# Norms by way of DRAM in the first layer and a ring of four pools in the third

## The chip, the cores and the metric

The kernel runs on one core of a Trainium2 chip. The metric is the time of one execution in microseconds on the device; the kernel before has a median of 5616.28 us over three runs (5610.35 to 5618.55). The profiled execution that is read here took 5603.3 us, with a span of 5601.4 us.

## What is computed

The input is a batch of two images of 512 channels and 64 x 64 pixels in float32. Four layers follow one another; each adds to its input what it makes of the group-normalised input.

1. A windowed attention with eight heads of 64 channels. Queries and keys are scaled to unit length per head and pixel; each pixel attends to its 3 x 3 neighbourhood and to 256 pooled tokens.
2. A deformable attention, in which keys and values are sampled at learned offsets.
3. An adaptive pooling. Each channel takes a mixture of its own maximum pools of sizes 1, 3, ... 13; the mixture follows from the channel's mean.
4. A linear attention with random features.

What the change touches is, cut to the core:

```python
# layer 0 (the "first layer")
k_l = k_l / max(norm(k_l), 1e-12)              # per head and pixel; q likewise
attn = softmax(concat([attn_local, attn_pool]))
x_local = einsum(lt, v_local)                  # nine neighbours, lt = learned + softmax weight
x_pool  = einsum(a_pool, v_pool)
# layer 2 (the "third layer")
gap   = mean(x, (2, 3));  s = relu(relu(gap @ w1.T + b1) @ w2.T + b2)
q_s   = clip(floor(s), 0, 5)
out   = frac_b * pools[q_s + 1] + frac_s * pools[q_s] + x
```

## The kernel before, in words

Channels lie on the 128 partitions, in four chunks. An image of 512 channels fills one of two big SBUF buffers; while one holds the image X, the other, Y, is working space.

**First layer (class Local).** The work is cut into 16 units per image: four chunks of 128 channels (two heads each) times four strips of 1024 pixels. `run` (L1739) is a software pipeline: in one turn of its loop, unit u attends (`attend`, L2123), unit u+1 has its tap products and tap sums made (`tap_products`, `tap_sums`) and its values projected, units u+3 and u+4 have queries and keys projected (`projections`), and unit u-1 is weighed (`weigh`, L2203). A tap is one of the nine neighbours. These stages are generators; `in_turn` takes one step of each in rotation. The tile framework then puts each engine's instructions in a fixed order by its own priorities, and every engine works through its list in that order. The transfers of this layer are all issued from one queue, that of SyncE (SP), also in order. "T" is used below for the start of one turn, at its sums of squares.

The norms of a turn come about as follows (`norms`, L1993). The squares of four half strips are summed per head by matmuls with a constant into rows 32s and 32s+1 of one PSUM bank (L2003), and ACT copies the bank to `rows` (L2006). Four transposes (L2010) put pixels on partitions, so that 128 x 32 numbers remain; the DVE takes reciprocal roots with a bit trick and three Newton steps (L2013 to L2024) into the zero-filled tile `wide`; four transposes (L2029) and a copy (L2031) bring them back to rows. `normed` (L2035) spreads each row over 64 partitions by a matmul (L2043) and multiplies the raw keys and queries (L2051). `learned` (L2057) then makes the query that the next turn uses.

The reciprocals of the softmax sums stay in `recip` (L2183). They weight the taps (L2186) and, in `weigh`, the attended values: two matmuls (L2213) spread them over the partitions and the DVE multiplies (L2216). The nine tap weights go to DRAM (`rows`, L2190) and from there to 64 partitions each (`fetch_tap`, L2196, two transfers of 256 KB per tap) into a ring of three buffers. For each tap ACT copies the weights to PSUM (L2223), the DVE multiplies the shifted values (L2226), and GpSimd adds to the output (L2230).

**Third layer.** `pool_weights` (L637, called from L1137) makes the group statistics and the mixture with small operations on the DVE, a power on GpSimd (L99) and a few matmuls. `pool_chunk` (L1140) then goes over the four chunks of channels. Each pool is the 3 x 3 maximum of the one before: a horizontal maximum into h, a vertical one into p (`spread_max`, L683: one DVE operation over 3968 columns, and ACT copies the edges). PE adds each pool, times a diagonal matrix of its weights (L1151), into eight PSUM banks (L1153). Y holds two h and two p buffers, so pool j+2 overwrites pool j. ACT then evacuates the banks and gathers the next layer's statistics (L1183, L1188).

Of the kernel before, what the change touches and what calls it, by code (L numbers as in the profile page):

```python
# [2 lines left out]

# [5 lines left out]
F32 = mybir.dt.float32  # L9
I32 = mybir.dt.int32  # L10
AF = mybir.ActivationFunctionType
ALU = mybir.AluOpType
# [3 lines left out]
P = 128  # L16
C = 512
KC = C // P
# [39 lines left out]
class General:  # L58
# [578 lines left out]
    def pool_weights(self, X, w1, w2, sp, pp, mv=None):  # L637


        nc, vec = self.nc, self.vec  # L640
        nmean, rstd, mv = self.group_stats(X, sp, pp, mv)
        gap = sp.tile([P, KC], F32, name="gap")
        nc.vector.tensor_tensor(gap, mv[:, :, 0], nmean, ALU.add)
        nc.vector.tensor_tensor(gap, gap, rstd, ALU.mult)
        ps = pp.tile([P, TB], F32, name="mm")
        for kc in range(KC):
            nc.tensor.matmul(ps[:32, :1], w1[:, kc, :], gap[:, kc:kc + 1], start=(kc == 0),
                             stop=(kc == KC - 1))
        mid = sp.tile([32, 1], F32, name="mid")
        nc.scalar.activation(mid, ps[:32, :1], AF.Relu, bias=vec[:32, V_B1:V_B1 + 1])  # L650
        ps = pp.tile([P, TB], F32, name="mm")
        for oc in range(KC):
            nc.tensor.matmul(ps[:, oc:oc + 1], w2[:, oc * P:(oc + 1) * P], mid, start=True,
                             stop=True)
        s, q, t, fb, fs = (sp.tile([P, KC], F32, name=f"pw_{n}") for n in ("s", "q", "t", "fb", "fs"))
        nc.vector.tensor_tensor(s, ps[:, :KC], vec[:, V_B2:V_B2 + KC], ALU.add)
        nc.vector.tensor_scalar(s, s, 0.0, None, ALU.max)

        nc.vector.tensor_scalar(q, s, 8.0, None, ALU.min)
        qi = sp.tile([P, KC], I32, name="pw_qi")  # L660
        nc.vector.tensor_copy(qi, q)
        nc.vector.tensor_copy(q, qi)
        nc.vector.tensor_tensor(t, q, s, ALU.is_gt)
        nc.vector.tensor_tensor(q, q, t, ALU.subtract)
        nc.vector.tensor_scalar(q, q, 5.0, None, ALU.min)
        nc.vector.tensor_tensor(fb, s, q, ALU.subtract)
        nc.vector.scalar_tensor_tensor(fs, q, 1.0, s, ALU.add, ALU.subtract)
        wts = sp.tile([P, 7, KC], F32, name="pw_w")
        for j in range(7):
            nc.vector.scalar_tensor_tensor(wts[:, j], q, float(j), fs, ALU.is_equal, ALU.mult)  # L670
            nc.vector.scalar_tensor_tensor(t, q, float(j - 1), fb, ALU.is_equal, ALU.mult)
            nc.vector.tensor_tensor(wts[:, j], wts[:, j], t, ALU.add)
        c0 = sp.tile([P, KC], F32, name="pw_c0")
        d0 = sp.tile([P, KC], F32, name="pw_d0")
        nc.vector.tensor_tensor(d0, fs, fb, ALU.add)
        nc.vector.scalar_tensor_tensor(d0, d0, 1.0, nmean, ALU.add, ALU.mult)
        nc.vector.tensor_tensor(d0, d0, rstd, ALU.mult)
        nc.vector.tensor_tensor(wts, wts, bcast(rstd, 1, 7), ALU.mult)
        nc.vector.tensor_tensor(c0, wts[:, 0], rstd, ALU.add)
        nc.vector.tensor_scalar(c0, c0, 1.0, None, ALU.add)  # L680
        return c0, d0, wts

    def spread_max(self, out, in_, axis):  # L683
# [244 lines left out]
class Net(General):  # L928
# [206 lines left out]
        return w  # L1135

    def pool_weights(self, X, w1, w2, sp, pp):  # L1137
        return super().pool_weights(X, w1, w2, sp, pp, self.mv)

    def pool_chunk(self, X, Y, cc, c0, d0, wts, sp, ppa):  # L1140

# [1 line left out]
        nc = self.nc  # L1143
        x2 = X[:, cc, :]
        img = x2.rearrange("p (y x) -> p y x", x=W)
        tmp = [Y[:, i, :].rearrange("p (y x) -> p y x", x=W) for i in range(KC)]
        accs = [ppa.tile([P, TB], F32, name="acc") for b in range(NB)]

        def add(w, src, j):
# [5 lines left out]

        add(c0[:, cc:cc + 1], x2, 0)
        for j in range(1, 7):
            h, p = tmp[j % 2], tmp[2 + j % 2]
            if j == 1:
                self.spread_max(h, img, 2)  # L1160
                nc.vector.tensor_tensor(h, h, img, ALU.max)
                self.spread_max(p, h, 1)
                nc.vector.tensor_tensor(p, p, h, ALU.max)
            else:

                self.spread_max(h, tmp[2 + (j - 1) % 2], 2)
                self.spread_max(p, h, 1)
            add(wts[:, j, cc:cc + 1], Y[:, 2 + j % 2, :], j)
        mv = self.mv[:, cc]
        if cc == KC - 1:  # L1170

# [488 lines left out]
class Local:  # L1660
# [9 lines left out]
    def __init__(self, net, X, Y, sp_scale, d, wp, yp, pp, ppt, pps):  # L1670
# [4 lines left out]

        self.yd = yp.tile([P, KC, N], F32, name="yd")
        self.wd = yp.tile([3, P, KC, C], F32, name="wd")
        self.rows = cycle([yp.tile([P // 2, self.UT], F32, name=f"rows{i}") for i in range(2)]).__next__

        R = W + 2  # L1680
# [30 lines left out]
        self.w3 = new([P, 3, KC, P], "w3")  # L1711
        self.sq = [new([P, TB], f"sq{i}") for i in range(4)]
        self.half = new([P, 32], "mhalf32")
        self.wide = new([P, NT, P], "wide")
        self.qb = new([P, KC], "qe_scaled")
        self.bias = {i: new([P, KC], "b_" + i) for i in "qkv"}
        self.raw = {"k": self.kraw, "q": self.qn}
# [6 lines left out]
            load(self.raw_w[i], d["W_kv"][:, i * C:(i + 1) * C])  # L1724
        nc.sync.dma_start(self.tok, d["tok32"])
        nc.vector.memset(self.half, -0.5)
        nc.gpsimd.memset(self.wide, 0.0)

        nc.vector.tensor_tensor(self.qb, self.vec[:, V_QE:V_QE + KC], sp_scale, ALU.mult)

# [262 lines left out]
    def norms(self, streams, ended):  # L1993
# [10 lines left out]
                             before[s % len(before)][4], start=True, stop=True)  # L2004
        rows = wp.tile([P, TB], F32, name="n_rows")
        nc.scalar.copy(rows, ps)  # L2006
        yield
        ps = self.bank()
        for t in range(NT):
            nc.tensor.transpose(ps[:, t * P:(t + 1) * P], rows[:, t * P:(t + 1) * P],  # L2010
                                self.net.ident)
        n, y, a = (wp.tile([P, NT, 4, 2], F32, name=f"norms{i}") for i in range(3))
        nc.vector.tensor_scalar(n, ps.rearrange("p (t s r) -> p t s r", t=NT, s=4)[:, :, :, :2],  # L2013
                                1e-24, None, ALU.max)
        yield

        nc.vector.tensor_scalar(y.bitcast(I32), n.bitcast(I32), 1, None, ALU.logical_shift_right)
        nc.vector.tensor_scalar(y.bitcast(I32), y.bitcast(I32), -1, 0x5f3759df, ALU.mult, ALU.add)
        nc.vector.tensor_scalar(n, n, -0.5, None, ALU.mult)
        for i in range(3):  # L2020
            nc.vector.tensor_tensor(a, y, y, ALU.mult)
            nc.vector.tensor_tensor(a, a, n, ALU.mult)
            dst = self.wide.rearrange("p t (s r) -> p t s r", s=4)[:, :, :, :2] if i == 2 else y
            nc.vector.scalar_tensor_tensor(dst, a, 1.5, y, ALU.add, ALU.mult)  # L2024
        yield
        yield
        ps = self.bank()
        for t in range(NT):
            nc.tensor.transpose(ps[:, t * P:(t + 1) * P], self.wide[:, t, :], self.net.ident)  # L2029
        rows = wp.tile([P, TB], F32, name="n_rows")  # L2030
        nc.scalar.copy(rows, ps)  # L2031
        ended += [(s, rows[32 * s:32 * s + 2, :], *a) for s, a in enumerate(before)]
        yield

# [88 lines left out]
    def attend(self, u):  # L2123
# [64 lines left out]
        self.spread = self.rows()  # L2188
        for j in range(2):
            nc.sync.dma_start(self.spread[:, j * TB:(j + 1) * TB], el[j * HD:(j + 1) * HD, :])  # L2190
        self.fetch_tap(0)
        yield
        self.fetch_tap(1)
        yield

    def fetch_tap(self, k):  # L2196

        at = 32 * (k % 2) + 2 * k
        for h in range(2):
            self.nc.sync.dma_start(self.taps[k % 3][h * HD:(h + 1) * HD, :],  # L2200
                                   bcast(self.spread[at + h], 0, HD))

    def weigh(self, u):  # L2203

        nc = self.nc
        cc, y0 = u // self.UN, u % self.UN * self.UY
        out, R = self.out.pop(u), self.recip
        self.fetch_tap(2)
        yield
        banks = [self.bank() for _ in range(2)]  # L2210
        for j, ps in enumerate(banks):
            q = slice(64 * j, 64 * j + 2)
            nc.tensor.matmul(ps, self.cst[q, C_ROW:C_ROW + P], R[q, :], start=True, stop=True)  # L2213
        for j, ps in enumerate(banks):
            o = out[:, j * TB:(j + 1) * TB]
            nc.vector.tensor_tensor(o, o, ps, ALU.mult)  # L2216
        for k in range(9):
            dy, dx = divmod(k, 3)
            parts = [self.taps[k % 3][:, j * TB:(j + 1) * TB] for j in range(2)]

            banks = [self.bank() for _ in range(2)]
            for ps, part in zip(banks, parts):
                nc.scalar.copy(ps, part)  # L2223
            for j, (ps, part) in enumerate(zip(banks, parts)):
                y = y0 + dy + j * self.UY // 2
                nc.vector.tensor_tensor(  # L2226
                    part.rearrange("p (y x) -> p y x", x=W),
                    self.vx[:, y:y + self.UY // 2, dx:dx + W],
                    ps.rearrange("p (y x) -> p y x", x=W), ALU.mult)
            nc.gpsimd.tensor_tensor(out, out, self.taps[k % 3], ALU.add)  # L2230
            if k + 3 < 9:
                self.fetch_tap(k + 3)
            if k < 8:
                yield
        lo = u % self.UN * self.UT
        nc.sync.dma_start(self.yd[:, cc, lo:lo + self.UT], out)
# [162 lines left out]
```

## Time and profile before

The page gives each engine's busy time over the whole span:

| engine | busy us | share | main work |
|---|---|---|---|
| PE (matmul) | 5235.5 | 93% | all projections, attention, pool additions |
| DVE | 3176.3 | 57% | elementwise work, maxima |
| ACT | 1790.9 | 32% | exponentials, copies |
| POOL (GpSimd) | 1811.4 | 32% | additions |
| DMA | | 16.5% of 16 engines | loads, tap weights |

By place in the first image: the first layer ends at about 1150 us of the span, the second at about 1625, the third at about 1910 and the fourth at about 2830; the second image repeats this.

A stage's row in the windows query names an engine's busy time within that stretch. In a timeline, a row's bracket tells how long the engine sat idle ahead of the instruction and which instruction released it. Matmuls in float32 are recorded as two each, so "x8" is four matmuls. Only time on an engine that something later waits for counts toward the end.

### The profile page before, as it was taken

What the parts mean: (1) busy time and instruction counts of PE and PEld (TensorE: products, weight loads), DVE (VectorE), ACT (ScalarE), POOL (GpSimd) and SP (SyncE); (2) the same over time, 40 slices, a digit from 0 to 9 for tenths busy, and PEclk for the clock granted to TensorE, in tenths of its full rate; (3) what the DMA queues carried; (4) which work ended last, traced back from release to release, by engine and by line L of the source; (5) the groups of instructions that cost most, each with busy time, mean ns of one, the idle gap of its engine ahead of it and who ended that gap; (6) DMA issues with size and microseconds to landing.
All of it is one profiled execution on the core that took longest, in us unless ns stands there. A gap on an engine that the chain in (4) does not pass through costs nothing.

```text
span 5601.4 us, 51804 instructions
## 1 busy us (share of the span) xinstructions
PE 5235.5 (93%) x19291; PEld 2262.8 (40%) x19291; DVE 3176.3 (57%) x3816; ACT 1790.9 (32%) x3413; POOL 1811.4 (32%) x1196
## 2 busy tenths in 40 slices
PE   7899999999978899999998999999999789999999
PEld 3433332555323444544343333325543334445443
DVE  3257777745669633544432677777456795334444
ACT  1245555333212233212212455542332122332221
POOL 0025555501310045444400455554012101453443
PEclk9899999999989999999998999999999899999999
DMA  3024444500000000201010344454000000000000
GB/s 138 0 64 119 122 115 136 167 21 24 1 1 0 1 1 1 76 18 36 31 51 2 84 117 116 119 145 143 17 24 1 1 0 1 1 8 14 18 16 24
DMA packets 103353, 276.37 MB, mean 49 GB/s; under 512 B 15090, under 2 KB 28146, under 8 KB 101044
## 3 DMA queue, kind: packets, MB, share of 16 engines
q1 hardware_dynamic: 103092, 272.97, 16.5%
q8 instruction: 154, 2.52, 0.2%
q14 instruction: 107, 0.88, 0.1%
HBM read 224.68 MB, written 48.23 MB: 49 GB/s over the span
## 4 chain that ended last, share of the span: by engine, by line
PE 72%; DVE 15%; issue 5%; DMA 3%; POOL 2%; ACT 2%; SPq 0%; DVEq 0%; ACTq 0%; POOLq 0%
PE mm L133 25%; DVE big L692 6%; PE mm L1330 4%; PE mm L1615 4%; PE mm L1370 4%; PE mm L547 4%; PE mm L1410 2%; PE mm L1226 2%; PE psO L1242 2%; PE psO L1602 2%; PE mm L1631 2%; PE tap L2104 2%; PE mm L1933 2%; POOL late L2230 2%; DMA big<-rows 2%
## 5 line engine op out<-in xcount | busy, mean ns | idle before, releaser
L133 PE MATMUL mm<-big,w 128*128 128x512 f32 x2560 | 1199.2, 613 | 6.5 <-DVE late L2183 5.0
L133 PEld LDWEIGHTS mm<-big,w 128*128 128x128 f32 x2560 | 469.6, 193 | 707.7 <-issue 602.0
L2230 POOL TENSOR_TENSOR late<-late,big 128x1024 f32<-128x1024 f32 x192 | 454.0, 2365 | 335.2 <-DVE big L2226 331.7
L1153 PE MATMUL acc<-big,dg 128*128 128x512 f32 x896 | 408.1, 614 | 79.6 <-DVE big L692 51.2
L692 DVE TENSOR_TENSOR big<-big 128x3968 f32<-128x3968 f32 x96 | 410.8, 4290 | 38.8 <-ACT big L693 16.7
L1232 POOL TENSOR_TENSOR total<-prob 128x512 f32<-128x512 f32 x128 | 159.7, 1270 | 758.4 <-ACT prob L1229 758.4
L1584 POOL TENSOR_SCALAR qf_sum<-qf,ksum_ratio 128x512 f32<-128x512 f32 x128 | 198.8, 1562 | 551.9 <-ACT qf L1634 351.7
L1405 POOL TENSOR_TENSOR big<-big 128x512 f32<-128x512 f32 x224 | 277.4, 1271 | 237.0 <-ACT big L1396 237.0
L2151 POOL TENSOR_TENSOR late<-late 128x512 f32<-128x512 f32 x128 | 160.5, 1275 | 502.5 <-ACT late L2140 477.2
L1609 DVE RECIPROCAL k<-psD 128x512 f32<-128x512 f32 x64 | 214.9, 3357 | 182.6 <-PE psD L1606 182.6
L1153 PEld LDWEIGHTS acc<-big,dg 128*128 128x128 f32 x896 | 174.0, 197 | 312.2 <-issue 282.5
L2223 ACT COPY mm<-big 128x512 f32<-128x512 f32 x384 | 221.7, 594 | 196.6 <-DMA big<-rows 103.3
L1396 ACT ACTIVATE big<-mm,ed 128x256 f32<-128x256 f32 x512 | 194.1, 489 | 278.0 <-DVE top L1392 250.3
L2226 DVE TENSOR_TENSOR big<-big,mm 128x512 f32<-128x512 f32 x384 | 252.4, 680 | 31.9 <-ACT mm L2223 30.9
L2230 POOL TENSOR_TENSOR late<-late,tap 128x1024 f32<-128x1024 f32 x96 | 228.0, 2375 | 122.0 <-DVE norms L2024 72.4
L1330 PE MATMUL mm<-proj,k 64*128 64x256 f32 x2048 | 265.6, 391 | 0.9 <-ACT k L1297 0.9
L1249 DVE RECIPROCAL recip<-psD 128x512 f32<-128x512 f32 x64 | 214.9, 3358 | 87.1 <-PE psD L1246 87.1
L2091 DVE TENSOR_TENSOR prod<-qs,big 128x1024 f32<-128x1024 f32 x192 | 231.0, 1218 | 42.9 <-PE tap L2104 42.6
L1551 DVE TENSOR_REDUCE tops<-mm 128x2 f32<-128x512 f32 x256 | 159.4, 681 | 165.1 <-PE mm L1330 165.0
L1229 ACT ACTIVATE prob<-mm 128x512 f32<-128x512 f32 x256 | 132.0, 604 | 364.4 <-PE mm L1226 359.2
L1330 PEld LDWEIGHTS mm<-proj,k 64*128 64x128 f32 x2048 | 207.8, 188 | 95.0 <-issue 78.7
L1615 PE MATMUL mm<-k,w 128*128 128x512 f32 x512 | 235.6, 602 | 0.0
(352 smaller groups left out, 8384.6 us busy)
## 6 DMA issues: line engine op xcount, KB each, us to landing
big<-rows SPq DMA_DIRECT2D x384, 256.0 KB, 4.0
tap<-rows SPq DMA_DIRECT2D x192, 256.0 KB, 4.1
yd<-late SPq DMA_DIRECT2D x32, 512.0 KB, 4.1
out<-big SPq DMA_DIRECT2D x64, 256.0 KB, 2.0
big<-in_W_kv SPq DMA_DIRECT2D x8, 1024.0 KB, 6.2
rows<-late SPq DMA_DIRECT2D x64, 128.0 KB, 2.4
big<-yd SPq DMA_DIRECT2D x16, 512.0 KB, 4.1
big<-in_x SPq DMA_DIRECT2D x4, 2048.0 KB, 7.6
```

The costliest lines, as they stand in the source:

```text
L133: self.nc.tensor.matmul(ps, w[:, kc, :], X[:, kc, blk * TB:(blk + 1) * TB], start=(kc == 0), stop=(kc == KC - 1))
L547: nc.tensor.matmul(ps, w[:, kc, oc * P:(oc + 1) * P], att[:, kc, :], start=(kc == 0), stop=(kc == KC - 1))
L692: nc.vector.tensor_tensor(o, a, b, ALU.max)
L1153: nc.tensor.matmul(accs[b], dg, src[:, b * TB:(b + 1) * TB], start=(j == 0), stop=(j == 6))
L1330: nc.tensor.matmul(pS[h][i][:, t, :], k[lo:lo + HD, tok:tok + P], proj[lo:lo + HD, :], start=True, stop=True)
L1370: nc.tensor.matmul(ps, X[:, kc, lo:lo + P], wv[:, kc, :], start=(kc == 0), stop=(kc == KC - 1))
L1405: nc.gpsimd.tensor_tensor(a, a, part, ALU.add)
L1615: nc.tensor.matmul(ps, self.wo[:, kc, oc * P:(oc + 1) * P], qs[:, kc, :], start=(kc == 0), stop=(kc == KC - 1))
L2091: self.nc.vector.tensor_tensor(self.prods[k % 3].rearrange("p (y x) -> p y x", x=W), qs, self.kx[:, y + dy:y + dy + self.UY, dx:dx + W], A ...
L2223: nc.scalar.copy(ps, part)
L2226: nc.vector.tensor_tensor(part.rearrange("p (y x) -> p y x", x=W), self.vx[:, y:y + self.UY // 2, dx:dx + W], ps.rearrange("p (y x) -> p y ...
L2230: nc.gpsimd.tensor_tensor(out, out, self.taps[k % 3], ALU.add)
```

## The change

The first layer's norms no longer go through the tensor engine for their change of layout. The rows of sums go to DRAM and come back spread over all 128 partitions as 128 x 32 numbers; the DVE works on them, with two intermediate tiles in PSUM; the results go back to rows by DRAM. The reciprocals of the softmax sums are treated as a tenth tap: row 20 of the weights holds them (the exponential of an empty tap sum is 1, its learned part 0), and they are fetched ahead of the nine others. So eight transposes, one ACT copy and two matmuls per turn disappear; six small transfers, two large ones and two ACT copies are added. The tile `wide` and its memset go.

In the third layer, the pools go round a ring of four buffers (three of Y's and a new one), with a single h. The statistics move from the DVE to ACT and GpSimd, and the maxima from the second pool on are queued behind the last operation of the mixture, in the first chunk. Both are meant to let PE begin its additions sooner and to keep the DVE from waiting for a buffer.

```diff
@@ norms
         rows = wp.tile([P, TB], F32, name="n_rows")
         nc.scalar.copy(rows, ps)
-        yield
-        ps = self.bank()
-        for t in range(NT):
-            nc.tensor.transpose(ps[:, t * P:(t + 1) * P], rows[:, t * P:(t + 1) * P],
-                                self.net.ident)
-        n, y, a = (wp.tile([P, NT, 4, 2], F32, name=f"norms{i}") for i in range(3))
-        nc.vector.tensor_scalar(n, ps.rearrange(...)[:, :, :, :2], 1e-24, None, ALU.max)
-        yield
+        self.flat.reverse()
+        sums, roots = self.flat[0]
+        every = lambda a: a.rearrange("h s (c e) -> (h s c) e", e=32)
+        for h in range(2):
+            nc.sync.dma_start(sums[h], rows[h:P:32, :])
+        n, y = (wp.tile([P, 32], F32, name=f"norms{i}") for i in range(2))
+        nc.sync.dma_start(n, every(sums))
+        yield
+        yield
+        ps = self.bank()
+        m, a = ps[:, :32], ps[:, 32:64]
+        nc.vector.tensor_scalar(m, n, 1e-24, None, ALU.max)
...
         for i in range(3):
-            nc.vector.tensor_tensor(a, y, y, ALU.mult)
-            nc.vector.tensor_tensor(a, a, n, ALU.mult)
-            dst = self.wide.rearrange(...)[:, :, :, :2] if i == 2 else y
-            nc.vector.scalar_tensor_tensor(dst, a, 1.5, y, ALU.add, ALU.mult)
-        yield
-        yield
-        ps = self.bank()
-        for t in range(NT):
-            nc.tensor.transpose(ps[:, t * P:(t + 1) * P], self.wide[:, t, :], self.net.ident)
+            nc.vector.tensor_tensor(a, m, y, ALU.mult)
+            nc.vector.tensor_tensor(a, a, y, ALU.mult)
+            nc.vector.scalar_tensor_tensor(y, a, 1.5, y, ALU.add, ALU.mult)
+        nc.sync.dma_start(every(roots), y)
         rows = wp.tile([P, TB], F32, name="n_rows")
-        nc.scalar.copy(rows, ps)
+        for h in range(2):
+            nc.sync.dma_start(rows[h:P:32, :], roots[h])
@@ fetch_tap, weigh
-        at = 32 * (k % 2) + 2 * k
+        at = 32 * ((i - 1) % 2) + 2 * (i - 1) if i else 20
...
-        banks = [self.bank() for _ in range(2)]
-        for j, ps in enumerate(banks):
-            q = slice(64 * j, 64 * j + 2)
-            nc.tensor.matmul(ps, self.cst[q, C_ROW:C_ROW + P], R[q, :], start=True, stop=True)
-        for j, ps in enumerate(banks):
-            o = out[:, j * TB:(j + 1) * TB]
-            nc.vector.tensor_tensor(o, o, ps, ALU.mult)
-        for k in range(9):
+        for i in range(10):
...
+                if i == 0:
+                    o = out[:, j * TB:(j + 1) * TB]
+                    nc.vector.tensor_tensor(o, o, ps, ALU.mult)
+                    continue
@@ pool_weights (third layer): on ACT instead of the DVE
+        nc.scalar.mul(nmean, ps[:, :KC], -1.0)
+        for kc in range(KC):
+            nc.scalar.activation(col(cent, kc), mv[:, kc, 0:1], AF.Identity, bias=col(nmean, kc))
+        nc.scalar.activation(var, cent, AF.Square)
+        for kc in range(KC):
+            nc.scalar.activation(col(var, kc), col(var, kc), AF.Identity, bias=mv[:, kc, 1:2])
...
+        nc.gpsimd.tensor_tensor(rstd, var, self.mhalf[:, :KC], ALU.pow)
+        for kc in range(KC):
+            nc.scalar.mul(col(gap, kc), col(cent, kc), col(rstd, kc))
@@ pool_chunk
-        tmp = [Y[:, i, :].rearrange("p (y x) -> p y x", x=W) for i in range(KC)]
+        if cc == 0:
+            self.pools = [Y[:, i, :] for i in range(1, KC)] + [sp.tile([P, N], F32, name="pool4")]
+        h = image(Y[:, 0, :])
...
-            h, p = tmp[j % 2], tmp[2 + j % 2]
+            flat = self.pools[(6 * cc + j) % KC]
+            p = image(flat)
...
-                self.spread_max(h, tmp[2 + (j - 1) % 2], 2)
-                self.spread_max(p, h, 1)
+                with self.tc.issue_after(self.mixed) if cc == 0 else nullcontext():
+                    self.spread_max(h, last, 2)
+                    self.spread_max(p, h, 1)
```

## The prediction

> **What bounds the kernel now.** I read the page's chain first, then busy time in windows of 50 us, then the timelines of one unit of the first layer and of the start of the third. The chain by engine, and one window inside the first layer's units (length, then PE, PEld, DVE, ACT, POOL busy, granted clock, DMA):
>
> ```profile
> PE 72%; DVE 15%; issue 5%; DMA 3%; POOL 2%; ACT 2%; SPq 0%; DVEq 0%; ACTq 0%; POOLq 0%
> ```
> ```profile
> 550.00:600.00 50.00, 47.62 (x172) 15.11 (x164) 35.90 (x50) 25.92 (x46) 26.22 (x13) 0.97 0.41 111
> ```
>
> The timeline of a unit on PE (start, length, instruction, idle before it):
>
> ```profile
> 799.62 1.13 PE L2213 MATMUL mm<-late,cst 2*128 2x512 f32 x4
> 800.86 0.66 PE L2010 MATMUL mm<-cst,n_rows 128*128 128x128 f32 x4
> ...
> 814.45 0.63 PE L2029 MATMUL mm<-cst,wide 128*128 128x128 f32 x4 [2.27 <-DVE wide L2024]
> ```
>
> PE ends most of the chain, and in a unit it is busy 47.6 of 50 us. Its one regular hole is 2.27 us ahead of the second set of transposes, L2029, which waits for the DVE's root. A unit without clock loss takes 48.32 us: L2003 starts at 749.25 and at 797.57. Four of 24 take 53.11, three about 50, and the twelve from 351.58 to 942.68 average 49.26. The reason shows in the timeline of a long one:
>
> ```profile
> 368.46 0.63 PE L2029 MATMUL mm<-cst,wide 128*128 128x128 f32 x4 [2.27 <-DVE wide L2024]
> 369.02 3.09 PE L2146 MATMUL mm<-late,vp 128*64 128x512 f32 x8
> ...
> 375.91 5.67 PE L133 MATMUL mm<-big,w 128*128 128x512 f32 x8
> ```
>
> After the same hole L2146 takes 3.09 instead of 1.94 us and L133 5.67 instead of 3.70. In the third layer the DVE ends the chain, but its first image plane stops once (timeline):
>
> ```profile
> 1652.59 5.12 POOL L99 TENSOR_TENSOR gn_rstd<-gn_var,cst 128x4 f32<-128x4 f32 x1 [42.44 <-DVE gn_var L97]
> ...
> 1660.80 0.16 DVE L656 TENSOR_TENSOR pw_s<-mm,vec 128x4 f32<-128x4 f32 x1 [2.89 <-PE mm L653]
> ...
> 1682.79 34.73 DVE L692 TENSOR_TENSOR big<-big 128x3968 f32<-128x3968 f32 x8 [16.71 <-ACT big L693]
> ```
>
> The third pool waits 16.71 us for a buffer that PE frees only after two additions, and PE starts late because small weight operations stand between maxima of 4.3 us.
>
> **The skill.** The Trainium skill, TensorE: Matmul & The Clock Gate, Part 1, says that PE falls to half its clock after an idle window of about 3.4 us; the rows above agree in kind, although 2.27 us was already enough now and then here. DMA: Bandwidth & Descriptors, Anatomy of one DMA, gives about 2.0 us fixed per transfer, mostly the write receipt; its section Queues, rings and completion order says that a later transfer's semaphore lands only after the earlier writes of the same DMA engine. The trace agrees on the first (DMA issues: size, median us to landing):
>
> ```profile
> row<-in_row SPq DMA_DIRECT2D x2, 64.0 KB, 1.7
> rows<-late SPq DMA_DIRECT2D x64, 128.0 KB, 2.4
> big<-rows SPq DMA_DIRECT2D x384, 256.0 KB, 4.0
> ```
>
> It shows no small transfer right behind a large one. GPSIMD Engine Reference, Specifications, says that GpSimd shares an SBUF port with DVE operations on two SBUF inputs. Here one L2022 takes 2.23 us beside others of 0.19:
>
> ```profile
> 810.94 0.19 DVE L2021 TENSOR_TENSOR norms<-norms 128x32 f32<-128x32 f32 x1
> 811.16 2.23 DVE L2022 TENSOR_TENSOR norms<-norms,norms 128x32 f32<-128x32 f32 x1
> ```
>
> **PE work per unit.** Removed are L2213 with its wait (799.62 to 800.86: 1.2), L2010 (0.67), L2029 (0.56) and the hole (2.27), about 4.7 us. Pure PE work becomes 43.5 us. If nothing else waited, that would be the unit. Added are two ACT copies of 0.59 less the one dropped (ACT has room, 26 of 50), two more tap transfers, and six small transfers, all on the one SP queue. I cost these by following the compiled order of the changed kernel with the old durations. T is the start of the sums of squares.
>
> **A first new wait.** Behind the sums PE has scores (1.06), five tap sums (1.8), values (1.87), the sums of tap 3 (0.98) and then those of tap 4. Product 3 on the DVE overwrites tap 0's buffer, so it waits for the first of the five sums, T+3.1. Behind it stand one reciprocal multiply (0.6), four weighings (0.6 each), product 4 (1.13): 1.13+0.6+2.4+1.13 puts product 4 at T+8.4. PE arrives at T+6.7: 1.8 us idle, and the sums of taps 3 and 4 no longer share the array, about 2.7 us in all.
>
> **The round trip.** Copy ends T+1.75; two writes and the read, which is issued about T+5, bring n by T+7.5, hidden. On the DVE the chain starts at T+9.5 behind product 5 and holds thirteen small operations (0.22 each when dependent), three products and two weighings; y is ready about T+16.4. The old 2.23 us does not return, since one operand is now in PSUM. But SP is in order: ahead of y's write are six fetches, the last two waiting for GpSimd's addition of tap 3 (2.4 us, ending T+15.9). So the write starts at T+17.05. It lands at T+19 (1.9, near the row of 1.7) or, behind the two 256 KB fetches that were just issued, at T+20.6 (their 4.0). I take the second, because of the ring order. Two reads back: 0.05+0.54+1.9, T+23.2. PE wants them for L2043 (L2079 in the new file) at T+20.3: 2.9 us idle. Everything behind is in order: 26.1 us of PE work to the next T. Unit: 49.3 us, with the bounds 47.6 (all transfers at 1.8) and 49.8.
>
> So +1.0 us on a quiet unit. Two holes of 1.8 and 2.9 us instead of one of 2.27 also invite the half clock more often: I put its mean loss at 1.2 instead of 0.95 us (49.26-48.32). That is +1.2 us for each of 24 units: **+29 us** (bounds -19 and +60).
>
> **First units.** In the iterations without attention nothing fills the round trip (PE timeline).
>
> ```profile
> 244.60 0.66 PE L2010 MATMUL mm<-cst,n_rows 128*128 128x128 f32 x4 [0.68 <-ACT n_rows L2006]
> 248.01 1.12 PE L2029 MATMUL mm<-cst,wide 128*128 128x128 f32 x4 [2.75 <-DVE wide L2024]
> 249.85 2.08 PE L2043 MATMUL mm<-n_rows,cst 2*128 2x512 f32 x4 [0.73 <-ACT n_rows L2031]
> ```
>
> From the end of the sums (243.9) to L2043 are 5.95 us. New: copy 0.75, issue 0.55, write 2.0, read 2.0, root 2.95, write 2.0, issue 0.55, read 2.0 and semaphores, 13 us: +7.1. The iteration before it has key heads to do meanwhile (+3.4). The one after reaches L2043 5.8 later but has 2 us of tap sums moved ahead (+3.8). The next gains 0.4. With PE already cold I add nothing: 14 us an image, **+28** (20 to 36).
>
> **Tail.** The last three units hang on fetches and GpSimd, not PE. Ten fetches instead of nine in a ring of three, about 2 us each, less 0.7 of PE work: **+8** (-4 to +16).
>
> **Third layer.** Statistics go to ACT (some 0.22 us a column) from 1635.2: first group sum, ten ACT operations, second sum and one more, 1639.0; the 5.12 us power, 1644.2; four columns, two matmul groups (0.56, 1.86), 1648.05. The compiled order puts the first weight operation ahead of the last maximum of pool 1, so the DVE idles from 1639.2 to 1648, does that maximum (4.4) and the rest of the weights (5.1): pool 2 starts at 1657.9. Ten more maxima at 4.39, and the next plane's first one: its second starts at 1706.2 instead of 1717.44, 11.2 us earlier. PE stays behind by one addition of 7 us, so four pools suffice. At each of three plane changes the DVE's sum over the statistics now stands before the last maximum of pool 1 and waits for ACT's 11.5 us of evacuation, about 0.6 each. Gain 9.4 an image: **-19** (-14 to -24). The dropped GpSimd memset costs nothing: it lay at the start, beside the loads.
>
> **Sum.** 29+28+8-19 = +46; 5616+46 = 5662 us.
>
> **Rivals.** *The round trip is hidden after all* (faster): small writes are not held by the fetches and holes shorten; units 47.5, no more clock loss, -0.8x24 = -19, start +20, tail 0, pools -22: 5595. For it: 1.7 us of the row transfer, and 4.7 us of PE work truly gone. Against it: the six fetches ahead of y's write, whatever a transfer takes. *Cancelling*: the units even, start +28 against pools -19 and some tail relief: 5616 within 11. *The clock gate takes over*: a hole near 3 us throttles every second unit, costing 5 us as in the rows above; 0.5x5-0.95 = 1.55 above the quiet +1.0, 2.55x24 = 61, with the rest 5694. For it: 2.27 us did it fully in four of the 24 units; against it: a throttle between the holes costs nothing, since PE waits anyway.
>
> **Chances.** Forecast 0.56, clock gate 0.13, cancelling 0.12, hidden 0.19. So faster 0.19, same 0.12, slower 0.69. The range 5590 to 5705 takes in all four cases' centres and the bounds of transfers, and leaves out a unit with no holes at all and one throttled always.
>
> **What would show it.** L2079 waiting 2 to 3 us for a DMA, tap sums waiting about 2 us for a product; T to T near 49; 13 us from sums to L2079 near 244 us; y's write landing in 3 to 4 us; the DVE's 16.71 us gone, about 9 us idle before L661 instead. A unit below 47.6, or no wait for the DMA at L2079, would mean that my order of SP or DVE is not what holds it.

## The result and the profile after

The changed kernel takes 5688.9 us (5688.2 to 5694.5 over four runs) against 5616.1 us before on the same chip (5610.4 to 5618.6): a ratio of 1.0133, with a 95% interval of 1.0116 to 1.0151. It is 73 us slower; 46 were forecast.

The trace allows a cut into stages. T0 is an image's first sums of squares (L2003 before, L2037 after), T4 those of the fifth turn, from which on the turns are full; T16 is twelve turns later. The third layer is taken from its first to its last maximum. Microseconds, first and second image:

| profiled run | T0 to T4 | twelve turns | T16 to third layer | maxima of third layer |
|---|---|---|---|---|
| before | 139.5, 139.5 | 591.1, 590.6 | 682.1, 681.9 | 272.6, 272.6 |
| after | 155.9, 154.2 | 614.9, 615.3 | 692.5, 692.0 | 258.1, 258.6 |
| difference, both images | +31.1 | +48.5 | +20.5 | -28.5 |
| forecast | +28 | +29 | +8 | -19 |

The differences add up to 71.6 us. The two profiled spans differ by 85.0; the rest is the fourth layer after the first image, which is 10.7 us longer in the changed kernel (more of this at the end), and some 3 us at the two ends of the span. (85.0 is more than 73 because the profiled run of before lies 13 us under its median.)

The window inside the units, after (length, then PE, PEld, DVE, ACT, POOL busy, granted clock, DMA):

```profile
550.00:600.00 50.00, 45.48 (x150) 13.46 (x149) 29.98 (x48) 26.04 (x46) 22.31 (x12) 0.97 0.47 118
```

The chain by engine, on the page after:

```profile
PE 16%; DVE 4%; issue 0%; POOL 0%; ACT 0%; DVEq 0%; ACTq 0%
```

It covers only the last fifth of the span (the shares add up to 20%), so it can't be held against the one of before; the windows and waits can. PE is busy 45.5 of 50 us, where it was 47.6: it has less to do and still takes longer. What it waited for between T4 and T16 of the first image, before and then after (us in total, times, longest):

```profile
PE mm L2029 <- DVE wide L2024: 27.2, 12, 2.3
```
```profile
PE mm L2079 <- DMA n_rows<-flat: 34.4, 12, 4.5
PE tap L2140 <- DVE prod L2127: 23.3, 12, 3.1
```

One hole of 2.27 us a turn has become two, 1.94 and 2.87 us in the mean. The PE timeline of a typical turn after, T = 729.17, shows both and what follows:

```profile
737.71 1.05 PE L2140 MATMUL tap<-prod,cst 128*32 128x512 f32 x4 [1.73 <-DVE prod L2127]
...
752.87 1.22 PE L2079 MATMUL mm<-n_rows,cst 2*128 2x512 f32 x4 [3.23 <-DMA n_rows<-flat]
754.01 5.40 PE L133 MATMUL mm<-big,w 128*128 128x512 f32 x8
```

L133 takes 5.40 us instead of 3.70: the half clock. In the same turn y is done at 745.57 (T+16.40); SP's own timeline then has

```profile
746.28 0.58 SPq L2062 DMA_DIRECT2D flat<-norms  x1
750.33 1.08 SPq L2065 DMA_DIRECT2D n_rows<-flat  x2
```

so the write starts 0.7 us after y, the reads start 4.05 us after the write, and L2079 another 2.5 us later, at T+23.70. From there to the next T are 27.75 us, of which 1.7 are the half clock: where L2079 to T ran at full clock it took 26.04.

The first units of the image: L2079 now waits, in PE's timeline,

```profile
260.59 2.08 PE L2079 MATMUL mm<-n_rows,cst 2*128 2x512 f32 x4 [11.69 <-DMA n_rows<-flat]
```

where the three rows of before had gaps of 0.68, 2.75 and 0.73 us. In the third layer (POOL's timeline, then the DVE's), the 16.71 us hole is gone:

```profile
1692.15 1.02 POOL L1161 TENSOR_TENSOR pool_rstd<-pool_var,cst 128x4 f32<-128x4 f32 x1 [3.77 <-ACT pool_var L1160]
...
1696.67 0.16 DVE L661 TENSOR_TENSOR pw_s<-mm,vec 128x4 f32<-128x4 f32 x1 [4.43 <-PE mm L658]
...
1706.20 4.29 DVE L697 TENSOR_TENSOR big<-big 128x3968 f32<-128x3968 f32 x1
```

The last row is the start of pool 2, 28.5 us after the layer's first maximum (1677.74), where 33.2 were forecast. (That the prediction has a 1706.2 too, on the clock of before, is chance.) The windows of this layer, before and after, settle where the gain is: the DVE is busy 248.5 us in both, and its idle time falls from 24.2 to 9.5.

```profile
1624.70:1897.40 272.70, 201.67 (x456) 87.44 (x454) 248.51 (x122) 61.94 (x177) 5.12 (x1) 0.89 0.00 1
```
```profile
1677.74:1935.80 258.06, 202.73 (x456) 87.68 (x454) 248.52 (x116) 64.47 (x190) 1.11 (x2) 0.92 0.01 1
```

### The profile page after: what moved, and what is told of

It is laid out like the page before. It is cut to its first block, busy times and chain, and to the rows that moved or that the text cites. A ratio compares the mean times of both kernels' runs of the same rounds, so it can differ in the third digit from the quotient of the medians.

```text
span 5686.4 us, 51600 instructions
## 1 busy us (share of the span) xinstructions
PE 5248.3 (92%) x18891; PEld 2258.6 (40%) x18891; DVE 3062.8 (54%) x3804; ACT 1805.6 (32%) x3471; POOL 1799.9 (32%) x1196
## 5 line engine op out<-in xcount | busy, mean ns | idle before, releaser
L133 PE MATMUL mm<-big,w 128*128 128x512 f32 x2560 | 1230.4, 628 | 8.6 <-DVE late L2219 7.1
L133 PEld LDWEIGHTS mm<-big,w 128*128 128x128 f32 x2560 | 486.8, 199 | 718.6 <-issue 642.4
L1182 PE MATMUL acc<-big,dg 128*128 128x512 f32 x704 | 317.6, 609 | 58.1 <-DVE big L697 27.2
L697 DVE TENSOR_TENSOR big<-big 128x3968 f32<-128x3968 f32 x72 | 308.8, 4289 | 6.6 <-DVE big L697 0.5
L2253 ACT COPY mm<-big 128x512 f32<-128x512 f32 x428 | 243.1, 597 | 160.4 <-DMA big<-rows 120.6
L2140 PE MATMUL tap<-prod,cst 128*32 128x512 f32 x768 | 199.9, 609 | 53.4 <-DVE prod L2127 52.0
L133 PE MATMUL mm<-big,big 128*128 128x512 f32 x512 | 243.2, 638 | 0.0
```

Of the source, the lines that this page charges most:

```text
L133: self.nc.tensor.matmul(ps, w[:, kc, :], X[:, kc, blk * TB:(blk + 1) * TB], start=(kc == 0), stop=(kc == KC - 1))
L697: nc.vector.tensor_tensor(o, a, b, ALU.max)
L1182: nc.tensor.matmul(accs[b], dg, src[:, b * TB:(b + 1) * TB], start=(j == 0), stop=(j == 6))
L2140: nc.tensor.matmul(ps[32 * q:32 * q + 32, :], self.cst[:, C_TAPW + 16 - 2 * k:C_TAPW + 48 - 2 * k], self.prods[k % 3][:, j * TB:(j + 1) * ...
```

## The experiments

**Each part alone.** Three kernels are the kernel before with some of the diff's hunks, so their diffs are those of the change: the third layer's hunks; all those of the first layer; and the first layer's split in two (the round trip of `norms`; the tenth tap of `fetch_tap` and `weigh`). Differences from before are taken from the ratio and the 5614.5 us of before in the same series.

> The kernel before with the third layer's part alone (ring of four pools, statistics on ACT and GpSimd, maxima held behind the mixture). Theory, from the trace after: the third layer gains about 15 us an image there, so 5616 - 30 = 5586 us, and the first layer is unchanged (units of 49.3 us). The prediction's own term says -19: 5597. Rival: the gain seen after is a later start of the layer that happened to fall well; then 5610 to 5620.

Measured: 5578.5 us, 0.9938 (0.9926 to 0.995), 35 us faster. Its maxima take 258.5 us in both images, as after, so 28 us of this are the layer's own.

> The kernel before with the first layer's part alone (norms by DRAM and the tenth tap). Theory: start-up 31, units 2.05 x 24 = 49, end of the layer 20, beginning 2: 5616 + 103 = 5719 us. Rival: the parts interact (the third layer's gain needs nothing of the first, but the reordered PE list of the first layer could be due to both): 5690 or less.

Measured: 5702.8 us, 1.0162 (1.0147 to 1.0177), +91 us. Start-up +31.0, turns +39.1, end +19.4. The start-up loss, the end and the third layer's gain are nearly the same apart and together, but the totals don't add: 0.9938 x 1.0162 is 1.0099, where the whole change measured 1.0133, 19 us more. In the profiled runs 9.4 us of this lie in the turns and 10.1 in the fourth layer, which no edit touches. Both go with the clock: with the whole change PE was at half clock for 112.6 us in the 24 turns and 78.5 in the fourth layer, with the first layer's part alone for 92.2 and 54.6. Why the clock fell more often isn't shown.

> Norms by DRAM, but the reciprocals are still spread by two matmuls and there are nine taps. Theory: the round trip makes the second hole (about 3 us ahead of the rows' spread) and the whole start-up loss of 31 us; the product that the tap sums wait for is late here too, by 1 to 2 us; a unit of 50.5 to 52 us, in all +65 to +100: 5680 to 5715. Rival: most of the unit's loss comes from the tenth tap's fetches on SP; then a unit of 49 us and 5640 to 5650.

Measured: 5640.4 us, 1.0052 (1.0037 to 1.0067), +29 us. Start-up 153.9 and 156.1, so the whole loss there is the round trip's. But the turns take 584.9 and 581.8, less than before. The full ones come almost only in two kinds, 47.4 to 48.1 us and 50.9 to 51.3. The size that I expected was too large. The total is the rival's (5640), and so nearly is the mean turn of 48.6 us, but not its reason: the tenth tap alone costs the turns nothing, as the next run shows. The profiled run is the fastest of four (5626.1), so the turns' gain may be smaller in the others.

> The tenth tap alone; norms still by transposes. Theory: 1.2 us of PE leave a unit, but products 3 and 4 slip behind the weighings, which wait for one more fetch, so that the tap sums wait 1 to 3 us: unit 49.3 to 51, the layer's end +10 an image, no start-up loss; 5630 to 5675. Rival: the first hole belongs to the round trip, and the tenth tap only takes PE work away: -1.2 x 24 = -29, 5587.

Measured: 5587.2 us, 0.9958 (0.9944 to 0.9973), 24 us faster, which is the rival's number, though its mechanism (no first hole) is not quite it. All full turns take 47.81 us. Its PE timeline:

```profile
789.21 1.04 PE L2104 MATMUL tap<-prod,cst 128*32 128x512 f32 x2 [1.37 <-DVE prod L2091]
...
796.91 0.63 PE L2029 MATMUL mm<-cst,wide 128*128 128x128 f32 x4 [0.97 <-DVE wide L2024]
```

There is a first hole, but it is short, the old one is shorter too, a third of 1.08 us follows (L133, for the DVE's L2225), and PE fell to half clock once in the twelve turns, for 3.4 us. The end of the layer is 11.9 and 9.0 us longer, as after: that loss is the tenth tap's.

So in the turns alone, -15 us (round trip) and -44 us (tenth tap), both images together, give +39 us when combined. The totals say the same: 1.0052 x 0.9958 is 1.001, and both together measured 1.0162. The traces show how. With the round trip alone the DVE typically reaches the root at T+7.95, y is ready at T+14.8, the rows (L2046 there, L2079 after) come at T+21.6, and PE, which still has the reciprocals' matmuls and stops 1.36 us for a product just ahead, arrives 0.3 us earlier (PE timeline of norms_only, T = 462.37):

```profile
483.98 1.22 PE L2046 MATMUL mm<-n_rows,cst 2*128 2x512 f32 x4 [0.30 <-DMA n_rows<-flat]
```

With the tenth tap the DVE's list has three products ahead of the root instead of one, and the root starts at T+9.53: y is 1.6 us later. PE arrives at T+20.5 instead of T+21.3, and waits 2.9 us. Each part used up the slack that the other needed.

**Taking the waits away.** In the first kernel L2079 reads a constant; in the second, two sums read a product that is there:

```diff
-        ended += [(s, rows[32 * s:32 * s + 2, :], *a) for s, a in enumerate(before)]
+        ended += [(s, self.fixed[32 * s:32 * s + 2, :], *a) for s, a in enumerate(before)]
```
```diff
-                                 self.prods[k % 3][:, j * TB:(j + 1) * TB], start=(k < 2),
+                                 self.prods[0 if k in (4, 5) else k % 3][:, j * TB:(j + 1) * TB], start=(k < 2),
```

> The changed kernel, in which L2079 reads a constant tile (0.1) in place of the roots, so nobody waits for the round trip; all its operations and transfers still run. Leaves out the division by the norms. Theory (two holes and the half clock that follows them make the unit): the second hole, 2 to 3 us, and its half clock go, the first hole stays: a unit of 47 to 48.5 us, and the start-up loss of 31 us goes: 5689 - 31 - 24 x 3.3 = 5580 (5560 to 5605). Rival (the unit is held by the products and the tap weights on DVE, ACT and SP, and the rows only happen to come at the same time): units stay above 50 us and only the start-up is won: 5640 to 5660.

Measured: 5496.7 us, 0.9792 (0.9775 to 0.9808), 192 us below the changed kernel. Turns of 44.3 to 45.3 us and few longer ones, twelve in 543.9; start-up 134.0. That is more than the theory gave, because the half clock nearly went with the wait (two stretches of 3.4 us in the twelve turns of the first image; 13 stretches, 54.6 us in all, after), and from L2081 to T it mostly took 25.85. PE's tap sums still wait for products, 20.8 us in the twelve turns. These holes now cost their length: turns of 44.3 us have one of 0.95, those of 45.3 one of 1.74. Less its hole a turn takes 43.4 to 43.6 us, the 43.5 of pure PE work that the prediction had.

> The changed kernel, in which the sums of taps 4 and 5 read product 3, which is there already, so the first hole has nothing to wait for. Leaves out the right sums of two taps; all products and sums still run. Theory: the round trip then sets the unit: y follows the weighings and copies as before, at most 1 to 2 us earlier, the second hole grows, and the unit falls only to 49.5 to 50.6 us: 5650 to 5675. Rival: each hole costs its own length, so 2.7 us a unit go: 48.5 us, 5624.

Measured: 5694.3 us, 1.0142 (1.0125 to 1.0159): no gain at all, less even than the theory gave. But the edit moved the first hole more than it removed it: the sums no longer wait, and about 1 us later L133 does, for ACT. In the twelve turns of the first image:

```profile
PE mm L133 <- ACT late L2176: 19.3, 12, 2.0
```

That is 19.3 us where the sums had waited 23.3. y is at T+16.4 in most turns as before, L2079 mostly at T+23.3 to 24.0, and the waits ahead of it have grown from 34.4 to 42.7 us. What PE saves ahead of the second hole it waits there, as long as the rows come no earlier: the first hole lies in the shadow of the second. The rival is not borne out, but with most of that hole still there the run is no clean test of it.

> Both edits together; leaves out what both leave out. Theory: PE has no hole left and runs at full clock: the prediction's 43.5 us of pure PE work, at most 45.5 with what DVE and transfers then hold; 5689 - 31 - 24 x 6.5 = 5500 (5470 to 5530). Rival (transfers and GpSimd hold the unit near 47.8, as the ring of three tap buffers allows): 5570 to 5580.

Measured: 5511.1 us, 0.9809 (0.9793 to 0.9826), near the theory's 5500, but PE is not without holes: L133 waits 13.2 us for ACT in the twelve turns here too, and the turns take 549.0 us, 5 more than with the rows' wait alone taken away. So a turn without the wait for the round trip takes 44.3 to 45.8 us.

**The half clock.** Two matmuls are put into the second hole:

```diff
+            for _ in range(2 if which == "k" and mine else 0):
+                nc.tensor.matmul(mine[0][1], self.cst[:, C_ROW:C_ROW + P], self.cst[:, :TB],
+                                 start=True, stop=True)
             for (s, rows, *_), ps in mine:
```

> The changed kernel with two more matmuls (128x128 times 128x512 of constants, into the bank that the first L2079 overwrites; about 1.85 us) in PE's list ahead of L2079, in the second hole. The result is unchanged. Theory (half clock after the holes costs 1.7 us a window): the second hole shrinks below 1.4 us, the half clock after it goes, a unit falls by 0.5 to 1.7 us: 5650 to 5677. Rival (the clock is not what holds the unit, since PE waits anyway): nothing is won, units stay at 51.2, 5685 to 5700.

Measured: 5670.2 us, 1.0101 (1.0082 to 1.0121), 19 us less than the changed kernel, inside the theory's range, but the half clock went only in some turns. In most it stayed, though PE was now idle for about 1 us only. PE timeline of such a turn (L2079 is here the filling, L2082 the rows):

```profile
848.24 1.98 PE L2079 MATMUL mm<-cst 128*128 128x512 f32 x4
850.15 1.04 PE L2143 MATMUL tap<-prod,cst 128*32 128x512 f32 x2
852.18 1.22 PE L2082 MATMUL mm<-n_rows,cst 2*128 2x512 f32 x4 [0.98 <-DMA n_rows<-flat]
853.33 5.40 PE L133 MATMUL mm<-big,w 128*128 128x512 f32 x8
```

Behind L2082 it stayed away in two turns of the first image and five of the second, and the rest of the turn took 25.97 to 26.06 us instead of 27.75. Over the 24 turns PE is at half clock for 75.1 us instead of 112.6; half of the 37.5 us between them is the gain. So the half clock does cost its 1.7 us, but the length of the hole just ahead does not decide whether it comes: a turn with 1.01 us of it ran at full clock, one with 0.83 did not.

**The trip itself.** One line, then another order:

```diff
-        nc.sync.dma_start(every(roots), y)
+        nc.scalar.dma_start(every(roots), y)
```

> The changed kernel with the write of the roots (L2062) issued from ACT's queue instead of SP's; nothing else. Theory (the prediction's: the write starts 0.7 us after y because SP is in order, and lands late because it stands behind two 256 KB fetches): it starts right at T+16.5 and lands in about 2 us, so L2079 comes at T+20.5 to 21.5 instead of T+23.3; the unit falls by 2 to 2.8 us where the half clock goes too, by 1.8 where it stays: 5689 - 24 x (1.8 to 2.8) = 5620 to 5645. Rival (the transfer's time is its own, whatever stands ahead): it starts 0.7 us earlier at most, and the reads still wait on SP for the sixth fetch; 5670 to 5689.

Measured: 5643.9 us, 1.0056 (1.0041 to 1.0072), 45 us less than the changed kernel, inside the theory's range but not by its sizes. In an ordinary turn (T = 713.43) ACT starts the write at T+16.66, just behind two fetches that SP has issued:

```profile
729.40 1.08 SPq L2238 DMA_DIRECT2D big<-rows  x2
730.09 0.33 ACTq L2062 DMA_DIRECT2D flat<-norms  x1
733.25 1.08 SPq L2065 DMA_DIRECT2D n_rows<-flat  x2
```

The reads follow 3.16 us later, not 2 (3.0 to 3.5 in the ordinary turns). In two turns of each image y is late and the write is issued just ahead of the fetches:

```profile
583.69 0.33 ACTq L2062 DMA_DIRECT2D flat<-norms  x1
584.21 1.08 SPq L2238 DMA_DIRECT2D big<-rows  x2
585.39 1.08 SPq L2065 DMA_DIRECT2D n_rows<-flat  x2
```

There the reads follow after 1.4 to 1.7 us, with the fetches' own issue in between. In the first turns of an image in the changed kernel, where no fetch is under way, it is 1.4 to 1.6 us. So the write alone is short, and it is late because it stands behind two large transfers, on another queue nearly as much as on theirs (3.5 to 4.05 us there). In ordinary turns L2079 comes at T+22.2 to 22.9, some 0.9 us earlier. The rest of the gain is clock: five of the first twelve turns ran the stretch from L2079 at full clock (26.0 to 26.1 us), and four of these took 48.3 to 48.8 us.

```diff
+            behind = self.scored.get((1, 0)) if k == 4 else None
+            with self.net.tc.issue_after(behind) if behind else nullcontext():
                 sums(k)
                 sums(k + 1)
```

> The changed kernel with the sums of taps 4 and 5 queued behind the scores of the next half (issue_after), so that PE has scores and a projection to do while product 4 is made; on the DVE this also lets the root's steps run nearly unbroken, y at about T+14.5. Theory (the unit is the time of y, plus 6.9 us of trip, plus 26 us of PE work, plus the half clock): L2079 at T+21.3, a unit of 47.4 at full clock and 49.1 with one half window: 5689 - 24 x (2.1 to 3.8) = 5600 to 5640. Rival (the holes only move: what PE saves at the first hole it waits at the second, y does not come earlier): 5680 to 5695.

Measured: 5694.4 us, 1.0152 (1.0136 to 1.0168): the rival's number, for another reason. In every other turn y is ready at T+14.4, as the theory had it, but its rows mostly come at T+21.0 to 21.5, and in the turns between at T+23.7 to 24.2 with y at T+14.8. SP in one turn of each kind (T = 678.25 and 729.68):

```profile
692.70 0.33 SPq L2062 DMA_DIRECT2D flat<-norms  x1
694.63 1.08 SPq L2241 DMA_DIRECT2D big<-rows  x2
695.82 1.07 SPq L2065 DMA_DIRECT2D n_rows<-flat  x2
...
740.76 4.28 SPq L2241 DMA_DIRECT2D big<-rows  x4
745.13 0.54 SPq L2062 DMA_DIRECT2D flat<-norms  x1
749.97 0.45 SPq L2241 DMA_DIRECT2D tap<-rows  x1
750.46 1.09 SPq L2065 DMA_DIRECT2D n_rows<-flat  x2
```

In the first, two fetches have slipped between write and reads, and the rows are used 3.8 us after the reads' issue began instead of 2.5; in the second the write follows two fetches directly, another fetch stands ahead of the reads, and 5.3 us pass from the write to them. On a queue shared with large transfers, an earlier y meets other fetches, and "y plus 6.9 us" is not a constant. It has more half clock besides (64.8 us from 365 to 950 us, where the changed kernel has 44.4).

**Versions.** The third layer's part and the tenth tap without the round trip; then the same with

```diff
-        self.fetch_tap(u, 0)
+        if u < self.direct:
+            self.fetch_tap(u, 0)
```

(`direct` is three less than the number of units) and the two matmuls of before for the last three units.

> The kernel before with the third layer's part and the tenth tap, norms still by transposes. Theory (the three parts' effects in different places add where the norms' round trip is not among them): 0.9938 and 0.9958 together, 5615 x 0.9896 = 5557 us, units at 47.8. Rival (the third layer's gain was partly clock chance in the first layer's units): 5570 to 5580.

Measured: 5571.0 us, 0.9927 (0.9913 to 0.9942), turns of 47.81 throughout. The profiled run is the fastest of five (5555.5), and its stages add nearly as the theory says: the end of the first layer is 5.7 us longer than with the tenth tap alone. The median lies at the rival's edge, 14 us above the theory. The five runs come in two groups, 5555.5 and 5557.2 at a granted clock of 0.968 to 0.969, and 5571.0 to 5578.3 at 0.965 to 0.966, so what parts the median from the theory goes with the clock.

> The third layer's part and the tenth tap, as in third_and_tenth, but the last three units of an image spread their reciprocals by matmuls as before, so their attended values need no transfer. Theory (the tenth tap's loss at the layer's end, 9 to 12 us an image from the last turn to the third layer's first maximum, comes from waiting for the tenth fetch): that stretch falls from 694 to about 684 us in both images, 20 us in all: 0.989 to 0.990 of before, about 5552. Rival (the loss comes from the longer ring of fetches and the bunching before the last turn, not from this wait): 690 us or more, 5565 to 5571.

Measured: 5547.9 us, 0.988 (0.9863 to 0.9896), the fastest of all, 67 us less than before. The stretch from T16 to the third layer takes 687.5 and 687.6 us, where the version above took 694.2 and 696.4: between the theory's 684 and the rival's 690. The waits of PE in the output of the first image (960 to 1090 us) say what went, third_and_tenth first:

```profile
PE mm L1966 <- DVE late L2255: 9.0, 1, 9.0
```
```profile
PE mm L1967 <- DVE late L2253: 4.2, 1, 4.2
```

The edit also takes the tenth fetch out of the ring for these units, and a wait of PE for the weighings falls from 4.5 us to 0.3 there. So it doesn't tell the value's own wait from the longer ring.

## Why the prediction was right, and where its sizes were off

*Slower, by about its mechanism: right.* The units lose by the round trip although PE has less work; this is shown by no_wait_rows, which removes the wait and nothing else of the trip and lies 192 us below the changed kernel (with the wait most of the half clock went too).

*The two holes: right.* The first was put at 1.8 us and is 1.73 in a typical turn; the second at 2.9 and is 2.87 in the mean. y at "about T+16.4" is T+16.40, the write at T+17.05 is T+17.1, the rows at T+23.2 are at T+23.1 to 23.7, and "26.1 us of PE work" is 26.04. The turn at full clock is thus the forecast 49.3. One turn in twelve ran so (49.12).

*The half clock in the units: the term that failed.* "I put its mean loss at 1.2 instead of 0.95." It is 1.7 us in nearly every turn; the means of all turns, 51.24 in the first image, lie 1.9 above 49.3. The rival that the clock gate takes over had the right total (5694) by a wrong picture: every second turn hit for 5 us, as in the rows of before. In its place: nearly every turn hit once, for one stretch of 3.4 us. The argument "a throttle between the holes costs nothing, since PE waits anyway" is no help, as the stretch lies behind the second hole, where nothing waits. This term is 20 us short in all. Some 9 of them are four turns (53.3 to 54.1 us, where the ordinary ones take about 51.3) in which the next weights (L1984, 256 KB) are fetched just ahead of T, and y comes 0.7 to 2.8 us later; the prediction didn't have them, and no run isolates that fetch.

*Why y's write lands late: right.* The 3.55 us were well sized (3.5 to 4.05 in ordinary turns), and so was the choice between a short landing and one behind the two fetches: ahead of them, or without them, the write takes 1.4 to 1.7. What the prediction left open is the queue. A write on ACT's queue behind the same fetches still takes 3.0 to 3.5, so their sharing SP's queue is the smaller part of the delay.

*First units: right in sum, with luck.* +28 was forecast and +31.1 measured; norms_only has all of it. Singly they are off, and the errors cancel: the turns lost 2.5, 4.9, 6.4 and 2.5 us in the first image, where 3.4, 7.1, 3.8 and a gain of 0.4 were forecast. In the second of these turns 11.7 us pass from the end of the sums to L2079, not 13; the write, put at 0.55 and 2.0 us, takes 1.57 from its issue to the reads'.

*Tail: mis-sized.* "Ten fetches instead of nine" gave 4 us an image; it is 10. The tenth fetch not only lengthens the ring: the attended value itself waits for it. PE's output projection L1967 waits for L2258 once for 9.95 us after, against 4.03 for L2216 before. tail_direct takes this away, with the tenth fetch of these units, and gets back 15.5 us of the 26.6 that third_and_tenth had lost there.

*Third layer: mis-sized.* +9.4 an image was forecast, 14.2 measured. The power was taken at the 5.12 us of before, but takes 1.02 us: in the profile before it ran beside maxima of the DVE, which now idles meanwhile. That fits what the Trainium skill says in GPSIMD Engine Reference, Specifications, of the SBUF interface shared with two-input DVE operations; no run isolates it. So L661 comes after an idle time of 4.43 instead of 8.8 us. The 0.6 us at each plane change did not appear: the DVE's list of waits has none of them.

## What to carry to other kernels

A transfer pair through DRAM in place of transposes is paid where its result is used: count the time from the last small operation to the use (here 7 us) and ask what the bounding engine has left to do meanwhile; saving work on that engine shortens what hides the trip. Test two parts of a change apart and together, since each can use up the slack that the other needs (here -15 and -44 us made +39). A small transfer that something waits for should be issued ahead of large prefetches; a queue of its own, behind them, gained some 0.9 us of the 7 here. A value that is needed first shouldn't come by a transfer where the pipeline has nothing left to hide it.

## What the runs showed of the hardware

- Half clock comes in stretches of 3.41 us (single or a few in a row), and turns of 51.0 to 51.3 us, close to fifteen such stretches (51.2), are what four different kernels fell into (after, first_only, norms_only, fill_hole), though their holes differ. norms_only has turns of 47.7 and of 51.1 us with the same holes, 0.17, 1.36 and some 0.3 us. That the two periods lock to each other is my reading; a plainer one fits as well, a turn at full clock and 1.7 us for each stretch (49.3 + 1.7, or 47.7 + 3.4). What triggers a stretch stays open. The Trainium skill's idle window of about 3.4 us (TensorE: Matmul & The Clock Gate, Part 1) is longer than any hole in these turns.
- A write of 16 KB from 128 partitions to DRAM took 1.4 to 1.6 us until a dependent transfer could be issued where no fetch was under way (after, first turns), 1.4 to 1.7 just ahead of two fetches of 256 KB (y_on_act), 3.0 to 3.5 just behind two on another queue (y_on_act) and 3.5 to 4.05 behind two on its own (after).
- The fourth layer (from the third layer's last maximum to T0 of the second image) took 1093.2 to 1094.1 us in six of the profiles and 1103.7 to 1104.4 in four, before and first_only among the former, after and y_on_act among the latter, and 1096.9 to 1100.1 in the others, without an edit there. The difference is clock: 54.6 to 58.0 us of half clock in the six, 78.5 in the four, and PE busy for 1073.4 us before and 1083.9 after with the same instructions. What decides it stays open, and it limits what one profiled run can say about 10 us. Runs of one kernel differ in the same way: norms_only took 5626.1 us at a granted clock of 0.958 and 5647.8 at 0.954.
